# A new order for a chain of four layers: the first stage's steps, the pooling passes, and the end of the last batch

## The chip, the cores and the metric

The kernel runs on one core of one Trainium2 chip. The metric is the time of one execution on the device in microseconds (us); lower is better. TensorE is called PE here, VectorE DVE, ScalarE ACT, GpSimd POOL, and SyncE, whose queue issues the transfers, SP, as in the profile.

## The reference, cut to what matters

The input x has 4 batches of 512 channels by 64 x 64 pixels, all in fp32. Four layers follow one another:

```python
# layer 0: attention over 4096 pixels with 64 channels
t = einsum('oc,bchw->bohw', w_qkv, x)             # 3*64 x 512: key, query, value
attn = softmax(einsum('bdk,bdq->bkq', key, query), axis=1)
x = scale * einsum('oc,bchw->bohw', w_out, einsum('bdk,bkq->bdq', value, attn)) + x
# layer 1: experts mixed by a router of the pooled x, then 1x1, 3x3 and 1x1 convolutions
rw = sigmoid(x.mean(axis=(2, 3)) @ router_w.T + router_b)
x = relu(bn(conv(relu(bn(conv(relu(bn(conv(x, w1))), w2))), w3)) + x)
# layer 2: linear attention
Q, K, V = softplus(Wq x), softplus(Wk x), Wv x
x = x + gamma * (Q (K V)) / (Q sum(K))
# layer 3: gates and a scan
p = einsum('bchw,oc->bohw', x, w_proj) + b_proj   # 1024 x 512: gate and scan half
s = ds_cumsum(ds_cumsum(p_scan, discount, axis=2), discount, axis=3)
x = x + gamma * p_gate * sigmoid(s)
```

`ds_cumsum` is y_t = d * y_(t-1) + x_t along an axis.

## The kernel before, in words

A batch is 4096 pixels, cut into eight blocks of 512; two neighbouring blocks are a pair, so that there are four pairs of 1024 pixels. x lies in five places of 128 x 4 x 1024, one for each pair and a spare one that serves as scratch. `unshifted` does everything; a loop over the batches calls `layer0`, `layer1`, `layer2` and `layer3`. The instructions of PE are in the order in which the program writes them down, throughout. Those of DVE and ACT are so only inside a `with tc.manual_schedule(...)` block that names the engine; elsewhere a scheduler places them. SP's queue is worked off in order, and an instruction on it that waits holds up those behind it.

**Before the first batch.** SP loads the projection weights `wqkv_sb` (L99), the four pairs of x (L92, L94: the first two in four chunks each), then a table of small parameters `prm` (L105) and other weights. DVE adds two parts of `wqkv_sb` (L103) and works out the scale and shift of the batch norms from `prm` (L152 to L158), with a square root on ACT in between (L153). POOL makes the identity matrix and scales `wv_sb` and `bv_sb` by a factor from `prm` (L120, L121).

**The first stage of layer 0** (class `Projections`, L208 on) makes keys, queries and values. Keys and queries come from a scheme of seven products for two pairs at a time, which needs sums and differences of the input and of the weights in place of an eighth product. `steps` (L225) gives the order as a string, one word for a step; the first string is for pairs 0 and 1, the second for pairs 2 and 3:

- A digit is one of the seven products: four instructions on PE, which the profile counts as eight matmuls (L296). Products 1, 6, 7 and 4 collect in the bank `y` (in the profile kq); 5, 2 and 3 go to the two halves of `zy` (kqz).
- "seed" copies `y` to the first half of `zy` after product 1, "e2" and "e3" copy it out after products 6 and 7. They are ACT's (L301, L304), and the next product into `y` waits for them.
- "c11" copies finished keys out (ACT, four copies, L282), "c12" adds the keys of the second pair (DVE, L310) and then copies them to the other half of the partitions (ACT, two copies); "c21" and "c22" write queries (DVE, L313, L315).
- "t" and "n" with a digit are DVE's two sums for a product (L244, `ring` in the profile), for this pair of pairs and for the next one.
- "v" with a digit is the value projection of a pair (L252), with "a" or "b" a half of it; "cp" copies values out on ACT (L258), "tr" transposes them on PE (L265) and copies them on DVE (L269).
- "zero", in batch 0 alone, is a product of the identity with a stretch of `wqkv_sb` that clears a bank.

**The attention loop.** For each of four pairs of query blocks there are 32 key tiles. `scores` makes a 128 x 1024 tile on PE (L354) into one of three buffers, ACT takes the exponential into a ring of twelve (L357), DVE adds it to a running sum (L360, L362), and `values` multiplies it on PE (L369). The loop goes by groups of six tiles: first the six scores of a group, then the six values of the group before. In each of groups 2 to 9 stands one call of `pool`, a copy of x in place on ACT with a sum (L431): 8 passes a batch, for the pooled mean. They are free for the scheduler to place. After group 0 of batch 0, `router_of_values` transposes the output weights on PE, copies them on DVE (L173) and multiplies them by the router (L175).

**Layer 3** goes over eight tiles. A tile is a pair and two of four channel blocks, with seven products for the scan half (`Sums`) and seven for the gate half (`Gates`), all at L904. A turn of the loop at the end of `layer3` weaves three things: the products of the `Sums` of tile i (letter s), the products of the `Gates` of tile i-1 (letter g), and the scan of tile i-1 (letter l: "rows" on DVE, "turn" on ACT, "columns" on DVE, "sigmoid" on ACT, for each of two channel blocks). `steps`, `first_steps` and `last_steps` give the order: "s5" is product 5 of the sums, "s seed" the copy after product 1, "copy_out 2" and "copy_out 3" the copies after 6 and 7, as above. "y" and "a" are the last products and additions of layer 2, "q" takes the next of its remaining parts, whose last is `divide` (PE L760, DVE L763), "t" sums for the next tile or batch, "v" the value projection of pair 0 of the next batch, "x" the load of its pair 3, "d" the factors of the column scan. The last turn has no sums. `Gates.third` and `second` call `add_x` (L981), which multiplies a 128 x 1024 result by gamma, adds x on DVE (L983) and issues the store on SP (L984).

At the very end a check of the softmax sums (`cnt` on PE, `fits` on DVE) is loaded by every engine, SP among them, and decides whether a second kernel, `general`, has to run; it does not.

Of the kernel before, what the change touches and what calls it, by code (L numbers as in the profile page):

```python
# [10 lines left out]
ALU = mybir.AluOpType  # L11
# [4 lines left out]
P = 128  # L16
# [9 lines left out]
E = 8  # L26
# [19 lines left out]
def unshifted(ctx: ExitStack, tc: tile.TileContext, fits, x, wqkv_t, wout_t, router_t,  # L46
# [52 lines left out]
    nc.sync.dma_start(wqkv_sb, wqkv_t.rearrange("(kc p) o -> p kc o", p=P))  # L99
    xs = [load_pair(0, pr) for pr in range(NPAIR)]  # L100

    a11, a12, a21, a22 = (wqkv_sb[:, k:k + 2, w * D:(w + 1) * D] for w in range(2) for k in (0, 2))
    nc.vector.tensor_tensor(a21, a21, a22, ALU.add)  # L103
    prm_sb = const.tile([P, NPRM], F32, tag="prm", name="prm_sb")
    nc.sync.dma_start(prm_sb, prm)  # L105
    def col(i, n=1):
        return prm_sb[:, i:i + n]

    wout_sb = const.tile([P, C], F32, tag="wout", name="wout_sb")
    for h in range(2):  # L110
# [14 lines left out]
    ones = const.tile([P, P], F32, tag="ones", name="ones")  # L125
    nc.gpsimd.memset(ones, 1.0)


# [37 lines left out]
    def router_of_values():  # L166


        wo_t = pair_psum("wo_t")
        wot_sb = block("wot_sb")  # L170
        for kc in range(KC):
            nc.tensor.transpose(wo_t[:, 0, kc * P:(kc + 1) * P], wout_sb[:, kc * P:(kc + 1) * P], ident)
        nc.vector.tensor_copy(wot_sb, wo_t[:, 0, :])  # L173
        for kc in range(KC):
            nc.tensor.matmul(wo_t[:, 1, 0:E], wot_sb[:, kc * P:(kc + 1) * P], router_sb[:, kc, :],  # L175
                             start=kc == 0, stop=kc == KC - 1)
        nc.vector.tensor_scalar(wr_sb, wo_t[:, 1, 0:E], col(SCALE), 1.0 / HW, ALU.mult, ALU.mult)

# [29 lines left out]
    class Projections:  # L208
# [3 lines left out]
        def __init__(self, b):  # L212
            self.b = b
            self.sums = bigp.tile([P, 4, 2, NB], F32, tag="big", name=f"ring_{b}")
            self.fours, self.vv, self.vsb = [], {}, {}

# [8 lines left out]
        def steps(self, b):  # L225
            first = "v1 cp01 v2 5 1 seed t6 t4 n5 6 e2 2 c11 n6 tr01 7 e3 c22 v3a n7 4 c21 3 c12 n4"
            if b == 0:
                first = "zero v0 1 seed t5 v1 cp01 t6 5 2 c11 t7 t4 n5 6 e2 n6 tr01 v2 7 e3 c22 v3a n7 4 c21 3 c12 n4"
            return first.split(), "5 1 seed 6 e2 2 c11 v3b cp23 7 e3 c22 tr23 4 c21 3 c12".split()

# [42 lines left out]
        def products(self, xs, pair, steps, key, qry, vt):  # L273
# [10 lines left out]
            for step in steps:  # L284
                if y is None and (step.isdigit() or step == "zero"):
                    y, zy = bank(f"kq_{self.b}_{pair[0]}"), pair_psum(f"kqz_{self.b}_{pair[0]}")
                if step == "zero":

                    nc.tensor.matmul(zy[:, 0, :], ident, wqkv_sb.rearrange("p k o -> p (k o)")[:, 0:NB],
                                     start=True, stop=True)  # L290
                elif step.isdigit():
# [15 lines left out]
                elif step == "c12":  # L307
                    for h in range(2):
                        r, n0 = slice(h * D, (h + 1) * D), (2 * pair[1] + h) * NB
                        nc.vector.tensor_tensor(key[r, n0:n0 + NB], zy[r, 1, :], e["e2"][r, :], ALU.add)  # L310
                    to_key(lambda h, n0: key[h * D:(h + 1) * D, n0:n0 + NB], pair[1], own=False)
                elif step == "c21":
# [15 lines left out]
    def layer0(b, xs, pro):  # L328
# [93 lines left out]
        def out_step(pr, m):  # L422
            add_out(pr, m, out_product(pr, m))
# [10 lines left out]
        late = []  # L434
        for g, group in enumerate(groups):
            for i in group:
                scores(i)
            if 1 < g < 2 + 2 * KC:
                pool(NPAIR - 2 + (g - 2) // KC, (g - 2) % KC)
            if g == 0:  # L440
                if b == 0:
                    router_of_values()
                continue
            for _ in range(2):
                if late and late[0][0] < g:
                    late.pop(0)[1]()
            for n, i in enumerate(groups[g - 1]):
                if g == len(groups) - 1 and n == 4:
                    inverse_sums(NPAIR - 1)
                pr = values(i)  # L450
                if pr is not None:
                    late.append((g, lambda pr=pr: sums(pr)))
                    if pr < NPAIR - 2:
                        late += [(g + 1, lambda pr=pr, m=m: out_step(pr, m)) for m in range(KC)]
        assert not [t for t in late if t[0] < len(groups) - 1], late
# [396 lines left out]
    def layer3(b, xs, value_product, value_add, left, weights, wcq):  # L852
# [109 lines left out]
        class Gates(Block):  # L962
            def first(self):
                s = self.half(0, 0)
                nc.vector.scalar_tensor_tensor(s, self.zy[:, 0, :], self.bias[0], s, ALU.add, ALU.mult)

            def fourth(self):
                nc.vector.tensor_tensor(self.e[3], self.zy[:, 1, :], self.e[3], ALU.add)

            def third(self):  # L970
                s = self.half(1, 0)
                nc.vector.scalar_tensor_tensor(s, self.x, self.bias[1], s, ALU.add, ALU.mult)
                nc.vector.tensor_tensor(self.half(1, 1), self.half(1, 1), self.e[3], ALU.mult)
                self.add_x(1)

            def second(self):
                nc.vector.tensor_tensor(self.e[2], self.zy[:, 1, :], self.e[2], ALU.add)
                nc.vector.tensor_tensor(self.half(0, 1), self.half(0, 1), self.e[2], ALU.mult)
                self.add_x(0)

            def add_x(self, i):  # L981
                m, s = self.j + 2 * i, self.s[i]
                nc.vector.scalar_tensor_tensor(s, s, col(GAM3), xs[self.pr][:, m, :], ALU.mult, ALU.add)  # L983
                nc.sync.dma_start(out[b, m * P:(m + 1) * P, self.pr * 2 * NB:(self.pr + 1) * 2 * NB], s)  # L984

# [5 lines left out]
        steps = (("s1", "s seed", "l rows 1"), ("g1", "g seed", "y", "l rows 0", "l turn 1"),  # L991
                 ("s5", "l turn 0", "a", "q"), ("g5", "l columns 1"),
                 ("s6", "s copy_out 2", "l columns 0", "y"), ("g6", "g copy_out 2", "l sigmoid 1", "a"),
# [5 lines left out]
                       ("s3", "s second"))  # L999
        last_steps = (("g5", "l rows 1", "l rows 0"), ("g1", "g seed"), ("g6", "g copy_out 2", "l turn 1"), ("g2",),  # L1000
                      ("g7", "g copy_out 3", "l columns 1", "g fourth", "l turn 0", "l columns 0", "l sigmoid 1",
                       "l sigmoid 0", "v"), ("g4",), ("g3", "x", "g third", "g first", "g second"))
        pro = None
        ys = [(pr, m) for pr in range(1, NPAIR) for m in range(KC)]
        nxt = []
        with tc.manual_schedule(engines={mybir.EngineType.DVE, mybir.EngineType.Activation}):
# [9 lines left out]
            for i in range(len(tiles) + 1):  # L1016
                who = {"l": last, "s": Sums(1, i) if i < len(tiles) else None, "g": Gates(0, i - 1) if i else None}
                made = None
                for step in first_steps if i == 0 else steps if who["s"] else last_steps:
                    for what in step:  # L1020
                        name, *args = what.split()
                        if what[0] in "sg" and what[1:].isdigit():
                            if who[what[0]]:
# [23 lines left out]
                        elif name == "v" and pro:  # L1047
                            pro.value(nxt, 0)
                        elif name == "x" and pro:
# [469 lines left out]
```

## Time and profile before

| | us |
|---|---|
| time, median of 3 runs | 2700.67 (2700.61 to 2700.9) |
| the profiled execution: time / span | 2700.49 / 2698.4 |
| PE busy | 2650.6 |
| DVE busy | 2013.2 |
| ACT busy | 1318.2 |
| POOL busy | 11.8 |
| first product of PE starts | 4.38 |
| first scores of batch 0 start | 56.63 |
| first values of batch 0 start | 76.36 |
| first scores of batch 1 start | 730.50 |
| last product of PE starts | 2684.60 |
| last operation of DVE starts | 2691.93 |

The page gives each engine's busy time; the list of waits says which engine's instruction at which line waited for which, how long in total, how often and at most; the timeline gives the instructions in order with their start, their busy time and in brackets the idle time before them and what ended it. A busy PE can be a PE at half clock: the granted clock stands in its own row.

### The profile page before, as it was taken

Reading aid. Unit: us, or ns where it says so; the run is one execution under the profiler, and the core shown is the slowest. Engines: PE = TensorE matmul, PEld = TensorE weight load, DVE = VectorE, ACT = ScalarE, POOL = GpSimd, SP = SyncE. Lnnn points to the kernel's source line nnn. Section 1 sums busy time; section 2 is a strip of 40 time slices with the busy share of each in tenths; the row PEclk is TensorE's granted clock in tenths of the full one; section 3 lists DMA queues with packets and bytes.
Section 4 is the critical chain, followed back from the end, with each engine's and each line's share of the span. In section 5 each row is a group of like instructions: output and inputs, shape, how many; then the busy total and the mean of one; then the engine's idle time right before and its main releaser. Section 6 shows DMA issues by size and latency. Waiting matters only on the chain.

```text
span 2698.4 us, 25783 instructions
## 1 busy us (share of the span) xinstructions
PE 2650.6 (98%) x10048; PEld 1114.0 (41%) x10048; DVE 2013.2 (75%) x2270; ACT 1318.2 (49%) x1511; POOL 11.8 (0%) x26
## 2 busy tenths in 40 slices
PE   7999999999999999999999999999999999999998
PEld 2333365344333346434433334543443333554443
DVE  5678766788678876678877878668886777856787
ACT  4555353545655435345565453535556555353545
POOL 1000000000000000000000000000000000000000
PEclk9999999999999999999999999999999999999999
DMA  5000210022200021002220002001121000210011
GB/s 190 1 1 1 102 32 1 16 90 82 94 1 1 1 102 32 1 24 101 78 78 1 0 1 102 32 1 59 66 84 72 0 1 1 102 32 0 32 47 48
DMA packets 34595, 115.17 MB, mean 43 GB/s; under 512 B 2976, under 2 KB 12192, under 8 KB 32928
## 3 DMA queue, kind: packets, MB, share of 16 engines
q1 hardware_dynamic: 34464, 113.43, 11.2%
q8 instruction: 81, 1.33, 0.2%
q14 instruction: 50, 0.41, 0.0%
HBM read 79.86 MB, written 33.55 MB: 42 GB/s over the span
## 4 chain that ended last, share of the span: by engine, by line
PE 89%; DVE 5%; ACT 4%; DMA 1%; issue 1%; SPq 0%; DVEq 0%; ACTq 0%
PE av L369 17%; PE s L354 17%; PE sx L904 14%; PE zy L904 10%; PE z L648 4%; PE c L623 4%; PE c L551 4%; PE c L600 3%; PE wv L822 2%; PE y L413 2%; PE g L724 2%; PE xtr L709 2%; PE kq L296 2%; PE c2e L600 2%; PE vv L252 1%; DVE s L937 1%
## 5 line engine op out<-in xcount | busy, mean ns | idle before, releaser
L354 PE MATMUL s<-qv,key 64*128 64x512 f32 x2048 | 466.9, 602 | 3.4 <-ACT ring L357 3.4
L362 DVE TENSOR_TENSOR acc<-acc,ring 128x1024 f32<-128x1024 f32 x312 | 381.7, 1223 | 95.0 <-ACT ring L357 65.2
L357 ACT ACTIVATE ring<-s 128x1024 f32<-128x1024 f32 x336 | 317.1, 1039 | 210.6 <-PE s L354 210.6
L369 PE MATMUL av<-ring,qv 128*64 128x512 f32 x1344 | 304.5, 595 | 0.0
L354 PEld LDWEIGHTS s<-qv,key 64*128 64x128 f32 x2048 | 188.6, 187 | 279.5 <-issue 171.0
L362 DVE TENSOR_TENSOR acc<-acc,x 128x1024 f32<-128x1024 f32 x168 | 205.6, 1224 | 102.5 <-ACT x L357 89.5
L357 ACT ACTIVATE x<-s 128x1024 f32<-128x1024 f32 x176 | 171.7, 1040 | 203.2 <-PE s L354 203.2
L904 PE MATMUL sx<-t,x 128*128 128x512 f32 x512 | 237.7, 598 | 3.3 <-ACT zy L909 2.5
L369 PEld LDWEIGHTS av<-ring,qv 128*64 128x64 f32 x1344 | 93.3, 137 | 198.6 <-issue 198.6
L369 PE MATMUL av<-x,qv 128*64 128x512 f32 x704 | 167.2, 598 | 0.0
L909 ACT COPY zy<-sx 128x512 f32<-128x512 f32 x64 | 36.5, 570 | 265.8 <-PE sx L904 256.3
L904 PEld LDWEIGHTS sx<-t,x 128*128 128x128 f32 x512 | 95.1, 190 | 133.3 <-issue 117.4
L954 DVE TENSOR_TENSOR_SCAN t<-x,t 128x512 f32<-128x512 f32 x128 | 148.8, 1209 | 1.6
L943 ACT COPY t<-s 128x1024 f32<-128x1024 f32 x64 | 127.5, 1992 | 42.0 <-DVE s L937 41.4
L937 DVE TENSOR_TENSOR_SCAN s<-wc,s 128x512 f32<-128x512 f32 x128 | 146.0, 1202 | 0.0
L913 ACT ACTIVATE e<-sx,prm_sb 128x512 f32<-128x512 f32 x128 | 86.9, 685 | 108.6 <-PE sx L904 108.6
L960 ACT ACTIVATE s<-t 128x1024 f32<-128x1024 f32 x64 | 125.6, 1988 | 12.0 <-DVE t L954 12.0
L904 PE MATMUL zy<-t,wq 128*128 128x512 f32 x256 | 119.3, 604 | 0.0
L904 PE MATMUL sx<-t,wq 128*128 128x512 f32 x256 | 117.0, 597 | 2.1 <-ACT e L913 2.1
L904 PE MATMUL sx<-x,wq 128*128 128x512 f32 x256 | 117.1, 596 | 0.0
L904 PE MATMUL zy<-x,x 128*128 128x512 f32 x256 | 116.2, 594 | 0.0
L648 PE MATMUL z<-x,wqk_sb 128*64 128x512 f32 x512 | 115.9, 597 | 0.0
(229 smaller groups left out, 3443.6 us busy)
## 6 DMA issues: line engine op xcount, KB each, us to landing
out_dram<-s SPq DMA_DIRECT2D x64, 512.0 KB, 2.6
x<-in_x_dram SPq DMA_DIRECT2D x14, 2048.0 KB, 8.6
ex<-in_packed_dram SPq DMA_DIRECT2D x4, 2048.0 KB, 7.5
ex<-in_experts_dram SPq DMA_DIRECT2D x4, 2048.0 KB, 7.8
wq<-in_wproj_t_dram SPq DMA_DIRECT2D x32, 256.0 KB, 5.0
ex<-in_packed_dram SPq DMA_DIRECT2D x4, 1536.0 KB, 6.1
ex<-in_experts_dram SPq DMA_DIRECT2D x4, 1536.0 KB, 6.6
x<-in_packed_dram SPq DMA_DIRECT2D x4, 1536.0 KB, 8.3
```

The lines of the kernel that those rows point to most:

```text
L354: nc.tensor.matmul(s[:, h, :], key[r, kt * P:(kt + 1) * P], qry[r, pr * NB:(pr + 1) * NB], start=True, stop=True)
L357: nc.scalar.activation(p, s, AF.Exp)
L362: nc.vector.tensor_tensor(accs[pr], accs[pr], p, ALU.add)
L369: nc.tensor.matmul(avs[pr][h * D:(h + 1) * D, :], vt[:, kt, :], ring[i % RING][:, h, :], start=kt == 0, stop=kt == NT - 1)
L551: nc.tensor.matmul(y[:, h, :], wc[:, kc, :], xs[pr][:, kc, h * NB:(h + 1) * NB], start=kc == 0, stop=kc == KC - 1)
L600: nc.tensor.matmul(y[:, lo - a:hi - a], u, v[:, lo:hi], start=dy == 1, stop=dy == 2)
L648: nc.tensor.matmul(z[h * D:(h + 1) * D, i, :], wqk_sb[:, kc, w * D:(w + 1) * D], xs[pair[i]][:, kc, h * NB:(h + 1) * NB], start=kc == 0, s ...
L904: nc.tensor.matmul(y, w[:, c, self.kind, self.j * P:(self.j + 1) * P], v[:, c, :], start=c == 0 and k in (1, 5), stop=c == 1, skip_group_c ...
L937: nc.vector.tensor_tensor_scan(self.half(i, h), along[:, self.j + 2 * i, :], self.half(i, h), 0.0, ALU.mult, ALU.add)
L943: nc.scalar.copy(self.t[i].rearrange("p (w r) -> p w r", w=W), self.s[i].rearrange("p (r w) -> p w r", w=W))
L954: nc.vector.tensor_tensor_scan(th, down[:, i, :], th, 0.0, ALU.mult, ALU.add)
L960: nc.scalar.activation(self.s[i].rearrange("p (r w) -> p w r", w=W), tw, AF.Sigmoid)
```

## The change

It has these parts:

1. `prm` is loaded before x, and the sum of two parts of `wqkv_sb` is written down later. "zero" multiplies the identity by itself instead of a stretch of `wqkv_sb`.
2. The step strings of the first stage have a new order, for batch 0 and for the others. The copies behind "c12" are put off: those of the first two pairs to a new step "k", those of the last two to group 0 of the attention loop, after its six exponentials (`key_copies`).
3. The attention loop is put under `manual_schedule` for ACT, so that the pooling passes stay where they are written down. `router_of_values` leaves its products for the end of group 1.
4. In `steps` of layer 3 the "q" moves from s5 to behind g5. In `last_steps` the "v" is split: half of the value projection behind g1, half where it was.
5. For the last batch the last two turns become one, `end_steps`: the sums of the last tile (s), the gates of the last but one (g), and the gates of the last tile (h). The last tile's results are finished and stored in halves of 512 columns (`last`); those of g go through two POOL operations instead of one of DVE (`on_pool`).

The instruction lists show what goes with it: on PE, `cnt` stands behind the last product instead of between the last tile's products; on SP, four stores of 128 x 512 in place of two of 128 x 1024, and the stores of g stand between those of h. On SP the load of `fits` now has one store behind it; before, it had two.

```diff
@@ before the first batch
     nc.sync.dma_start(wqkv_sb, wqkv_t.rearrange("(kc p) o -> p kc o", p=P))
-    xs = [load_pair(0, pr) for pr in range(NPAIR)]
...
-    nc.vector.tensor_tensor(a21, a21, a22, ALU.add)
     prm_sb = const.tile([P, NPRM], F32, tag="prm", name="prm_sb")
     nc.sync.dma_start(prm_sb, prm)
...
+    xs = [load_pair(0, pr) for pr in range(NPAIR)]
...
     nc.gpsimd.memset(ones, 1.0)
+    nc.vector.tensor_tensor(a21, a21, a22, ALU.add)
@@ router_of_values
-        for kc in range(KC):
-            nc.tensor.matmul(wo_t[:, 1, 0:E], wot_sb[:, kc * P:(kc + 1) * P], router_sb[:, kc, :],
-                             start=kc == 0, stop=kc == KC - 1)
-        nc.vector.tensor_scalar(wr_sb, wo_t[:, 1, 0:E], col(SCALE), 1.0 / HW, ALU.mult, ALU.mult)
+
+        def products():
+            wr = pair_psum("wr_p")[:, 0, 0:E]
...
+        return products
@@ Projections.steps
-            first = "v1 cp01 v2 5 1 seed t6 t4 n5 6 e2 2 c11 n6 tr01 7 e3 c22 v3a n7 4 c21 3 c12 n4"
+            first = "v1 cp01 5 1 seed v2 t6 t4 n5 6 n6 e2 2 7 e3 c11 c22 tr01 n7 4 c21 3 c12 n4"
             if b == 0:
-                first = "zero v0 1 seed t5 v1 cp01 t6 5 2 c11 t7 t4 n5 6 e2 n6 tr01 v2 7 e3 c22 v3a n7 4 c21 3 c12 n4"
-            return first.split(), "5 1 seed 6 e2 2 c11 v3b cp23 7 e3 c22 tr23 4 c21 3 c12".split()
+                first = "zero v0 1 seed t5 v1 cp01 t6 5 2 t7 t4 6 e2 v2 7 e3 c11 c22 tr01 n5 n6 n7 4 c21 3 c12 n4"
+            return first.split(), "5 1 seed k v3a 6 e2 2 v3b cp23 7 e3 c11 c22 tr23 4 c21 3 c12".split()
+
+        def key_copies(self):
+            while self.left:
+                self.left.pop(0)()
@@ Projections.products
-                    nc.tensor.matmul(zy[:, 0, :], ident, wqkv_sb.rearrange("p k o -> p (k o)")[:, 0:NB],
-                                     start=True, stop=True)
+                    nc.tensor.matmul(zy[:, 0, :].rearrange("p (j c) -> p j c", c=P), ident,
+                                     ident[:, None, :].to_broadcast([P, TPB, P]), start=True, stop=True)
...
-                    to_key(lambda h, n0: key[h * D:(h + 1) * D, n0:n0 + NB], pair[1], own=False)
+                    self.left.append(lambda: to_key(lambda h, n0: key[h * D:(h + 1) * D, n0:n0 + NB], pair[1],
+                                                    own=False))
+                elif step == "k":
+                    self.key_copies()
@@ the attention loop
+        with tc.manual_schedule(engines={mybir.EngineType.Activation}):
+            for g, group in enumerate(groups):
...
+                if g == 0:
+                    pro.key_copies()
+                    if b == 0:
+                        router = router_of_values()
+                    continue
...
+                if b == 0 and g == 1:
+                    router()
@@ Gates (first, third and second now call add_x for each half)
+            last = on_pool = False
+
+            def add_x(self, i, h):
+                if h == 0 and not self.last:
+                    return
+                m = self.j + 2 * i
+                part = slice(h * NB if self.last else 0, (h + 1) * NB)
+                s = self.s[i][:, part]
+                if self.on_pool:
+                    nc.gpsimd.tensor_scalar(s, s, col(GAM3), None, ALU.mult)
+                    nc.gpsimd.tensor_tensor(s, s, xs[self.pr][:, m, part], ALU.add)
+                else:
+                    nc.vector.scalar_tensor_tensor(s, s, col(GAM3), xs[self.pr][:, m, part], ALU.mult, ALU.add)
...
@@ the orders of layer 3
-                 ("s5", "l turn 0", "a", "q"), ("g5", "l columns 1"),
+                 ("s5", "l turn 0", "a"), ("g5", "l columns 1", "q"),
...
-        last_steps = (("g5", "l rows 1", "l rows 0"), ("g1", "g seed"), ("g6", "g copy_out 2", "l turn 1"), ("g2",),
+        last_steps = (("g5", "l rows 1", "l rows 0"), ("g1", "g seed", "v 0"), ("g6", "g copy_out 2", "l turn 1"), ("g2",),
...
+        end_steps = (("s1", "s seed", "l rows 1"), ("g1", "g seed", "l rows 0", "l turn 1"), ("s5", "l turn 0"),
+                     ("s6", "s copy_out 2", "l columns 1"), ("g5", "l columns 0"),
+                     ("s2", "l sigmoid 1", "l sigmoid 0", "s first"), ("s7", "s copy_out 3", "s fourth"),
+                     ("g6", "g copy_out 2"), ("s4", "s third", "s rows 1", "d"),
+                     ("s3", "s second", "s turn 1", "s rows 0"), ("h1", "h seed", "s turn 0"), ("g2", "g first"),
+                     ("h5", "s columns 1"), ("g7", "g copy_out 3", "g fourth"),
+                     ("h6", "h copy_out 2", "s columns 0", "s sigmoid 1"), ("h2",), ("g4", "g third", "s sigmoid 0"),
+                     ("h7", "h copy_out 3", "h first", "h fourth"), ("g3", "g second"), ("h4", "h third"),
+                     ("h3", "h second"))
...
+                if b == B - 1 and i >= len(tiles) - 1:
+                    if i == len(tiles):
+                        break
+                    who["h"] = Gates(0, i)
+                    who["h"].last = who["g"].on_pool = True
```

## The prediction

> **What bounds the kernel now.** I read the page first: how busy each engine is.
>
> ```profile
> PE 2650.6 (98%) x10048; PEld 1114.0 (41%) x10048; DVE 2013.2 (75%) x2270; ACT 1318.2 (49%) x1511; POOL 11.8 (0%) x26
> ```
>
> TensorE (PE) is busy for all but 47.8 us of the 2698.4 us span. The change removes no product of weight, so it can only win gaps of PE, time in which PE runs at half clock, and the time after PE's last product. So the second view is the list of PE's waits over the whole run (us in total, times, longest).
>
> ```profile
> PE kq L296 <- ACT kqz L301: 7.5, 7, 2.8
> PE nrm L760 <- DVE x L827: 4.7, 4, 1.2
> ...
> PE kq L296 <- ACT e L304: 3.8, 5, 0.8
> PE s L354 <- ACT ring L357: 3.4, 4, 0.9
> PE wo_t L175 <- DVE wot_sb L173: 3.3, 1, 3.3
> ...
> PE sx L904 <- ACT zy L909: 2.5, 4, 0.7
> PE kqz L296 <- DVE qv L315: 1.8, 1, 1.8
> ```
>
> Seven, five and four times: the first stage of each of the four batches has the same small gaps, with larger ones in batch 0. The third view is the timeline of batch 0's start, PE, then ScalarE (ACT), then VectorE (DVE):
>
> ```profile
> 30.59 1.94 PE L296 MATMUL kq<-ring,wqkv_sb 128*64 128x512 f32 x8 [0.59 <-ACT e L304]
> 34.35 1.94 PE L296 MATMUL kqz<-x,kqw 128*64 128x512 f32 x8 [1.82 <-DVE qv L315]
> ...
> 42.57 3.51 PE L296 MATMUL kq<-ring,kqw 128*64 128x512 f32 x8 [2.85 <-ACT kqz L301]
> ```
> ```profile
> 28.43 0.21 ACT L153 ACTIVATE bn_s<-bn_v 128x6 f32<-128x6 f32 x1 [3.82 <-DVE bn_v L152]
> 28.66 1.28 ACT L331 ACT_TABLE_LOAD   x1
> 29.95 0.58 ACT L304 COPY e<-kq 128x512 f32<-128x512 f32 x1
> ```
> ```profile
> 26.97 1.23 DVE L244 TENSOR_TENSOR ring<-x,x 128x1024 f32<-128x1024 f32 x1 [5.45 <-DMA x<-in_x_dram]
> ...
> 34.21 4.08 DVE L244 TENSOR_TENSOR ring<-x 128x1024 f32<-128x1024 f32 x2
> ```
>
> See here: the copy e3 stands on ACT behind a square root, that behind bn_v on DVE, that behind the load of pair 3 (26.97). At 42.57 PE had waited 2.85 us and eight passes took 3.51 us, not 1.72. The last view is the end:
>
> ```profile
> 2684.60 1.92 PE L904 MATMUL zy<-x,x 128*128 128x512 f32 x4
> ```
> ```profile
> 2691.93 1.28 DVE L983 SCALAR_TENSOR_TENSOR s<-s,prm_sb,x 128x1024 f32<-128x1024 f32 x1
> ```
>
> PE ends at 2686.5, DVE at 2693.2; the last store is issued at 2693.3 and 5.1 us later the span ends.
>
> [...] The trace shows it after only 2.85 us: granted clock 0.50 from 43 to 45 us. [...] the first of the two sums at 34.21, beside POOL's 128x2048 scaling, took 2.94 us, the second 1.18. [...]
>
> **Batch 0's start, part by part.** Unit: a step of four instructions (eight passes) is 1.72 us, a value projection 3.43.
>
> - The clearing product "zero" needs only ident (POOL, done 1.4) instead of wqkv. No gain: PE then waits for the chunks of x, which came in at 8.01, 9.30, 10.58. A loss: PE is idle again until 6.3, so v0 starts at half clock. [...] I take 0.8.
> - prm moves ahead of x on SP's queue: everything behind it is one issue (0.5) and 25 KB later; I take 0.4 of delay (0.1 to 0.5).
> - The bn arithmetic and the square root go to the front of DVE and ACT. Cost nothing: DVE sits idle from 6.6 to 11.92 for x, ACT to 13.4. It takes 0.9 us and two table loads (2.6 us) off the stretch 23 to 32.
> - New step order, followed through: last chunk of pair 1 at 16.1, v1 to 17.0; 5, 2, 6 to 22.2; v2 to 25.6; 7 to 27.4; transposes to 28.3; 4, 3 to 31.7, no wait (copies e2, e3 of 0.58 now each have a product or the transposes beside them, and c22 comes at 28.0). Second pair: 5, 1, v3a to 36.9. Step 6 needs n6, and DVE does n5, n6, n7 only now: n5 to 32.2, then POOL's scaling (31.61 in the trace)[...], n6 to 38.4, so 6 ends at 39.3; 2, v3b to 42.7. Step 7 needs e2, queued on ACT behind the key copies "k", which need c12, on DVE behind n7 (40.7) and c21: 42.6, copies 43.25, e2 43.8. So 7 to 45.6, transposes, 4, 3 to 50.0. Scores start there, against 56.63.
> - Group 0: before, twelve scores and the router took 56.63 to 76.36 = 19.7 us, with waits of 0.85 and 3.35 us. The router's products now come a group later (0.5 us there); the two key copies (1.2) after exponential 5 make ACT fall behind by about a product. 12 x 0.905 + 0.55 + 0.4 = 11.8: values at 61.8, not 76.4.
>
> 14.5 - 0.5 - 0.8 = 13.2 us (10 to 15).
>
> **The pooling passes** (8 a batch, 1.06 + 0.19 us each) leave the first stage and go one to a group of the attention loop. Cost nothing: a group of six key tiles takes PE (466.9 + 471.7)/512 x 6 = 11.0 us, ACT's six exponentials 488.8/512 x 6 = 5.7. The pass comes after them, and the next scores are 5.5 us off.
>
> **The change of batch, three times.** Before, gaps of 0.66 (g seed), 0.67, 0.87, 0.79 and 0.85 us, and some 0.2 at each restart. In the new order v0's first half stands behind g1, v2 between seed and 6, v3a behind the second seed, "2" or v3b behind each e2, and ACT has no pooling passes. Followed through from the end of the last gate: scores start 4.0 us earlier, exponential 0 waits for nothing (+0.85), and the key copies after exponential 5 cost 0.7. 4.1 each (3 to 5), 12.4 together. n5 still waits for pair 3 (702.5) but is needed only at 709.7.
>
> **divide moved behind g5**, four times: nrm waited 1.18 us for a buffer that DVE frees at 2495.97; behind g5's 1.72 it is free. The product wv after it then waits about 0.3 for nrm's own buffer. 3.9 us in all (3 to 4.7).
>
> **The end.** 21 products of 1.72 from 2648.3. Copy_out 3 of the sums stands on ACT behind l sigmoid 0 (62.98) and s first, so s4 waits 2 us; PE ends at 2686.6 as before. But the chain rows, turn, columns, sigmoid now runs under h's products: s sigmoid 0 is done at 2680.9, and after h3 DVE has 2 to 3 us left. Against that, g's two results (g third done 2681.2) get gamma and x on POOL: twice a scaling and an add of 1024. Scaling: 6.2 us for 2048 and 1.92 for 512 give 3.35 on a line; [...] I take 2.8. [...] SP's order puts h's stores and the load of fits behind g's second store: three issues of 0.35 and 0.9 for fits, so the last issue is at about 2695.0 against 2693.3. A loss of 2 us[...]. cnt now comes after h3 and fits on DVE before three of h's last four operations: inside that count.
>
> **Sum**, against this execution (2698.4 span; it ran 2700.49, the three others 2700.61 to 2700.9): 13.2 + 12.4 + 3.9 - 2 = 27.5. 2700.67 - 27.5 = 2673.2.
>
> **Rivals.**
> - Half the first stage's gain: whatever ends a gap is followed by the next (n6 under POOL's scaling, "k" ahead of e2 on ACT, pair 3's load). For it: DVE's and ACT's queues are fixed, and my margins there are under 1 us. Against: most of the gaps before stand behind ACT work that leaves the stage. 13 us less: 2686.
> - POOL sets the end more dearly: adds and scalings of 3.35 us and more[...]. For it: the 2.94 us sum. End +8: 2679.
> - The end gains[...], and every gap closes: 2664.
> - Slower: the pooling passes hold up the exponentials, hence PE. 32 passes x 1.25 = 40 us against the 29.5 gained elsewhere than at the end: 2713. It decides from the point where ACT has under 1.25 us to spare in a group of six. Against: 5.3 us to spare.
> - The change does nothing: the gaps lie with loads. Only batch 0's first 17 us do; then about 2699.
>
> **How the numbers follow.** Forecast 0.55 (own range 2668 to 2679), half the gain 0.18, POOL's end 0.14, all gaps closed 0.08, slower 0.03, nothing 0.02. The range 2664 to 2684 leaves out the last two and a part of the half case. Faster by over 0.2% (5.4 us, about what a measurement of this kernel can tell from no change) has 0.95, within 0.02, slower 0.03.
>
> **What would show it.** Right: scores of batch 0 starting near 50 and their values near 62; no wait of kq for e or kqz of a microsecond; nrm without its 1.2; ACT's pooling passes between exponentials with no PE wait; four POOL instructions at the end, the last store behind them. Wrong: a clock of 0.5 in the first stage, waits of s for ring in the groups that pool, POOL instructions over 4 us, or kq waiting for ring sums between 32 and 45.

## The result, and the profile after

The changed kernel takes 2687.86 us (median of six, 2686.23 to 2688.84) against 2700.35 for the kernel before: a ratio of 0.9953, interval 0.9940 to 0.9966. It is 12.5 us faster, where 27.5 were forecast and the range ended at 2684. The profiled execution is the fastest of the six, 2686.23 with a span of 2684.4, so the two traces differ by 14.0 us.

The page's line of busy times for the changed kernel:

```profile
PE 2646.9 (99%) x10048; PEld 1113.4 (41%) x10048; DVE 2013.0 (75%) x2270; ACT 1314.6 (49%) x1510; POOL 23.9 (1%) x30
```

Its list of PE's waits (us in total, times, longest):

```profile
PE kqz L304 <- DVE qv L326: 6.2, 8, 0.8
PE sx L919 <- ACT e L928: 4.0, 9, 1.9
PE vv L260 <- DMA x<-in_x_dram: 3.9, 1, 3.9
PE s L365 <- ACT x L368: 3.1, 3, 1.0
...
PE kqz L304 <- DVE ring L252: 1.3, 1, 1.3
PE s L365 <- DVE wot_sb L173: 1.2, 1, 1.2
```

What the change aimed at is gone: kq waiting for kqz (7.5), for e (3.8), nrm (4.7) and wo_t (3.3; the scores now wait 1.2 us for the same copy `wot_sb`). But three other rows are new or grown. Kqz for qv was 1.8 us and is 6.2, eight times: it is product 3 of both halves of all four batches, waiting for c22. The scores wait for x, three times, at the key copies. Sx for e has one wait of 1.9, in the new end.

The timeline of batch 0's start, PE:

```profile
7.39 6.62 PE L260 MATMUL vv<-x,wqkv_sb 128*64 128x512 f32 x16 [3.87 <-DMA x<-in_x_dram]
...
33.12 1.94 PE L304 MATMUL kqz<-x,kqw 128*64 128x512 f32 x8 [0.76 <-DVE qv L326]
36.36 2.12 PE L304 MATMUL kqz<-ring,wqkv_sb 128*64 128x512 f32 x8 [1.30 <-DVE ring L252]
...
67.08 3.65 PE L380 MATMUL av<-ring,qv 128*64 128x512 f32 x16
```

and beside it ACT's four key copies c11, DVE's c22 and n5, and POOL's scaling:

```profile
29.99 2.35 ACT L290 COPY key<-kqz 64x512 f32<-64x512 f32 x4
```
```profile
32.38 0.69 DVE L326 TENSOR_TENSOR qv<-kqz,e 128x512 f32<-128x512 f32 x1 [10.30 <-PE kq L304]
...
34.18 3.17 DVE L252 TENSOR_TENSOR ring<-x,x 128x1024 f32<-128x1024 f32 x2
```
```profile
31.42 5.44 POOL L119 TENSOR_SCALAR wv_sb<-wv_sb,prm_sb 128x2048 f32<-128x2048 f32 x1 [29.95 <-DMA bv_sb<-in_bv_dram]
```

See three losses in a row: v0 takes 6.62 us, where the next two value projections take 3.62 (its passes take 1.06 us in the median instead of 0.59; that this is half clock was the author's reading, for the row of the granted clock reads 1.00 here); c22 starts only when c11 has ended (29.99 + 2.35); and n5, behind it, stands beside POOL. The first values start at 67.08, 9.3 us earlier than before, not 14.5.

The end, POOL, then the last of DVE, then the last of PE:

```profile
2664.99 2.85 POOL L1008 TENSOR_SCALAR s<-s,prm_sb 128x1024 f32<-128x1024 f32 x1 [265.31 <-DVE s L990]
2667.92 2.85 POOL L1009 TENSOR_TENSOR s<-s,x 128x1024 f32<-128x1024 f32 x1
2670.75 3.80 POOL L1008 TENSOR_SCALAR s<-s,prm_sb 128x1024 f32<-128x1024 f32 x1
2674.64 2.34 POOL L1009 TENSOR_TENSOR s<-s,x 128x1024 f32<-128x1024 f32 x1
```
```profile
2674.73 2.80 DVE L1011 SCALAR_TENSOR_TENSOR s<-s,prm_sb,x 128x512 f32<-128x512 f32 x1
```
```profile
2668.34 1.88 PE L919 MATMUL zy<-x,x 128*128 128x512 f32 x4
```

Two numbers split the 14.0 us of the traces. When product 1 of the last turn starts, the changed kernel is 17.2 ahead (2631.05 against 2648.29); from there to the end of the span it takes 53.35 instead of 50.1. So the last turn gives back 3.2.

### The profile page after: what moved, and what is told of

It reads as the page before. It is cut to its first block, busy times and chain, and to the rows that moved or that the text cites. A ratio compares the mean times of both kernels' runs of the same rounds, so it can differ in the third digit from the quotient of the medians.

```text
span 2684.4 us, 25795 instructions
## 1 busy us (share of the span) xinstructions
PE 2646.9 (99%) x10048; PEld 1113.4 (41%) x10048; DVE 2013.0 (75%) x2270; ACT 1314.6 (49%) x1510; POOL 23.9 (1%) x30
## 4 chain that ended last, share of the span: by engine, by line
PE 89%; DVE 5%; ACT 4%; issue 1%; DMA 0%; SPq 0%; ACTq 0%; DVEq 0%
PE av L380 17%; PE s L365 16%; PE sx L919 14%; PE zy L919 10%; PE z L663 4%; PE c L638 4%; PE c L566 4%; PE c L615 3%; PE wv L837 2%; PE y L424 2%; PE g L739 2%; PE xtr L724 2%; PE vv L260 2%; PE c2e L615 2%; PE kq L304 1%; PE kqz L304 1%
## 5 line engine op out<-in xcount | busy, mean ns | idle before, releaser
L975 ACT ACTIVATE s<-t 128x1024 f32<-128x1024 f32 x64 | 125.6, 1987 | 11.8 <-DVE t L969 11.7
L919 PE MATMUL zy<-x,wq 128*128 128x512 f32 x256 | 115.9, 592 | 0.0
```

The costliest lines, as they stand in the source:

```text
L919: nc.tensor.matmul(y, w[:, c, self.kind, self.j * P:(self.j + 1) * P], v[:, c, :], start=c == 0 and k in (1, 5), stop=c == 1, skip_group_c ...
L975: nc.scalar.activation(self.s[i].rearrange("p (r w) -> p w r", w=W), tw, AF.Sigmoid)
```

## The experiments

The experiments ran on three chips, each beside the kernel before: it took 2700.51 there for E1 to E4, 2699.90 for E5 and E7 to E9, and 2699.65 for E6 and E10 to E12. The changed kernel has one set of six times, beside 2700.35. The differences named below are differences of the times as they stand, and between chips up to 0.9 us of them can be the chip's. An interval of a ratio is about 3.5 us to either side; still, no run of E4 to E12 was as slow as the fastest of the changed kernel. The traces are compared by two numbers: where batch 0's first values start, and how long it is from there to the end of the span. The second leaves batch 0's start out.

| kernel | time, us | ratio to before, interval | first values | from there to the end |
|---|---|---|---|---|
| before | 2700.35 | | 76.36 | 2622.0 |
| changed | 2687.86 | 0.9953 (0.9940 to 0.9966) | 67.08 | 2617.3 |
| E1 c22 first | 2690.85 | 0.9968 (0.9956 to 0.9981) | 65.13 | 2620.0 |
| E2 clearing product four times | 2687.74 | 0.9953 (0.9939 to 0.9966) | 68.53 | 2617.8 |
| E3 prm later | 2686.96 | 0.9951 (0.9937 to 0.9964) | 68.49 | 2617.6 |
| E4 end on VectorE | 2685.01 | 0.9945 (0.9932 to 0.9959) | 69.23 | 2613.5 |
| E5 old end | 2683.88 | 0.9941 (0.9928 to 0.9955) | 69.68 | 2614.1 |
| E6 key copies later | 2682.30 | 0.9938 (0.9924 to 0.9951) | 69.06 | 2613.2 |
| E7 c11 early | 2683.06 | 0.9937 (0.9923 to 0.9950) | 68.51 | 2612.7 |
| E8 scaling on ScalarE | 2683.91 | 0.9942 (0.9929 to 0.9956) | 64.60 | 2617.5 |
| E9 = E7 + E8 | 2675.81 | 0.9915 (0.9902 to 0.9929) | 62.80 | 2611.1 |
| E10 = E9 + E4 + E6 | 2670.15 | 0.9892 (0.9877 to 0.9907) | 62.10 | 2605.4 |
| E11 = E10 + E3 + E12's order | 2666.38 | 0.9878 (0.9863 to 0.9893) | 61.60 | 2602.3 |
| E12 = E4 + copy ahead of sigmoid | 2682.90 | 0.9936 (0.9923 to 0.9950) | 69.24 | 2612.1 |

### E1, c22 ahead of c11

```diff
-  ... 7 e3 c11 c22 tr01 ...
+  ... 7 e3 c22 c11 tr01 ...        (all three strings)
```

> The changed kernel with one edit: in the three step strings c22 stands before c11. In the profile of the changed kernel c22 (DVE) starts each time when ACT's four key copies c11 end, and product 3 waits 0.77 us for c22, eight times. Theory A, c11 ahead of c22 is the cause: the eight waits (6.2 us, and some 0.2 at each restart) go, and in batch 0 the sums n5 to n7, which stand behind c22 on DVE, come 2.3 us earlier, so that product 5's wait of 1.3 us goes too: 7 to 10 us less than the changed kernel, that is 2678 to 2681. Rival, something else holds c22 or the next wait takes its place (key copies after exponential 5, n6 under POOL's scaling): 2 us less or nothing.

The median is 3 us slower than the changed kernel, and its six runs lie widely (2686.89 to 2695.92), for which the one trace, of the fastest run, gives no cause; that stays open. In batch 0 the half of theory A that concerns n5 came true: n5 starts at 30.91, takes 2.35 us, product 5 starts at 34.00 without a wait, and the values come 2 us earlier than in the changed kernel. From there on the trace is 2.7 us slower. PE's waits show what happened to product 3:

```profile
PE kqz L304 <- ACT key L290: 8.8, 8, 1.6
```

The eight waits are still there, and longer by 2.6 us in all; only the releaser has changed, from c22 to c11. Both copies read the tile zy, one its first half and one its second. Written in the order c11, c22, the second waits for the first (in the changed kernel's batch 0 c11 ends at 32.34 and c22 starts at 32.38); in the order c22, c11, product 3, which writes into zy, waits for c11 (0.91 us in batch 0). Product 3 waits for the last reader of the tile, whichever it is, and the four key copies (2.35 us) behind e3 make it late. That it is the shared tile which ties the two copies together is read from who releases whom in both orders; two separate tiles were not tried.

### E2, the clearing product issued four times

```diff
+  for _ in range(4):
       nc.tensor.matmul(zy[:, 0, :]..., ident, ident..., start=True, stop=True)
```

> The changed kernel with one edit: the clearing product zero is issued four times, so that PE is busy from 1.45 us until x arrives. Theory B, the first value projection lost its time to PE's halved clock after 3.9 us of idleness: its 16 passes end near 12.3 instead of 13.84 and all that follows comes 1 to 2 us earlier: 2686 to 2687. Rival, the chunks of x pace it: v0 ends where it did, and the time stays within 0.3 us.

PE is now busy from 1.45 to 7.83, and v0 takes 3.97 us instead of 6.62. Product 1 starts at 11.56, 2.3 us earlier than in the changed kernel's trace, whose v0 was a slow one: against the mean of ten traces with the same first instructions (12.76) it is 1.2, so about that is what the idle PE ahead of v0 costs. The time is unchanged, 2687.74, and the first values come at 68.53, later than in the changed kernel: product 5 of the second pair waits 3.13 us for n5 and starts at 36.10, as late as in the changed kernel (36.36).

### E3, prm behind the first two blocks of x

```diff
-  nc.sync.dma_start(prm_sb, prm)
-  xs = [load_pair(0, pr) for pr in range(NPAIR)]
+  xs = [load_pair(0, pr) for pr in range(2)]
+  nc.sync.dma_start(prm_sb, prm)
...
+  xs += [load_pair(0, pr) for pr in range(2, NPAIR)]
```

> The changed kernel with one edit: prm is loaded behind the chunks of pairs 0 and 1 instead of ahead of them. Theory C, the 25 KB in 128 short pieces cost the first chunk of x a microsecond (7.39 against at most 6.35 before): PE starts v0 1 us earlier, and the time falls by 0.5 to 1.2 us. Rival, the chunk was late for another reason, or the batch norm arithmetic, now behind t6 on DVE, holds up what follows: 0, or up to 1 us more.

V0 starts at 5.98 instead of 7.39, and product 1 at 11.27 instead of 13.84. The median is 0.9 lower, as theory C would have it, but the runs overlap (2685.78 to 2687.88 here), and in the trace nothing comes of the gain: product 5 waits 3.74 us for n5 and starts at 36.23, and the values come at 68.49. E2 and E3 together say that something pins that product at about 36 us, whatever PE wins ahead of it.

### E4, the closing additions on VectorE

```diff
-  who["h"].last = who["g"].on_pool = True
+  who["h"].last = True
```

> The changed kernel with one edit: on_pool stays False, so that g's two results of the last turn are finished by DVE in one operation each. Theory D, POOL's four operations (11.8 us one after the other) and the DVE operations that they block (four of 512 columns took 1.21, 1.99, 1.41 and 2.80 us instead of 0.67) set the end: DVE's last operation takes 0.7 us and the last store is issued 3 to 5 us earlier, so 3 to 5 us less: 2683 to 2685. Rival, the end is set by the chain of the last tile on DVE anyway, and two more operations of 1.28 us there cost as much as POOL did: within 1 us.

It is 2.9 us faster than the changed kernel, and the last turn takes 49.4 us instead of 53.35. Without POOL beside them DVE's four closing halves take 0.75 us each:

```profile
2677.23 0.75 DVE L1011 SCALAR_TENSOR_TENSOR s<-s,prm_sb,x 128x512 f32<-128x512 f32 x1
```

With POOL they took 1.21, 1.99, 1.41 and 2.80. After PE's last product DVE ends 5.5 us later instead of 7.3; and the last store is issued in the same moment (2678.0) instead of 1.9 us after DVE's end, where SP had still to send g's second store and to load fits (1.08 us). That makes 3.7 of the 4.0.

Its first stage is that of the changed kernel, and yet its values come 2.2 us later. PE is 1.75 us earlier at product 1 (12.09 against 13.84) and then waits longer:

```profile
37.01 3.31 PE L304 MATMUL kqz<-ring,wqkv_sb 128*64 128x512 f32 x8 [3.69 <-DVE ring L252]
```

The stretches of 2 us there (first the stretch and its length, then busy us and instructions of PE, weight loads, DVE, ACT and POOL, then the granted clock, the share of the DMA engines and GB/s):

```profile
36.00:38.00 2.00, 0.99 (x4) 0.23 (x4) 2.00 (x3) 0.00 (x0) 2.00 (x2) 0.86 0.02 8
38.00:40.00 2.00, 2.00 (x6) 0.79 (x6) 2.00 (x2) 0.00 (x0) 2.00 (x1) 0.50 0.00 0
```

The longer wait is followed by a granted clock of 0.50, and that costs another 1.7 us (products 5 and 1 take 3.03 and 2.12 us from start to start instead of 1.72). E4, E5, E6 and E12 have the same instructions up to the attention as the changed kernel, and in all four PE waits 2.0 to 3.9 us here, takes 5.1 to 5.4 us for products 5 and 1 together (in E6 too, whose clock was read, it was 0.50 from 38 to 40 us), and reaches the values at 69.1 to 69.7; E2 and E3, with waits of 3.1 and 3.7, do so at 68.5. The changed kernel's own trace has a wait of 1.30 and 67.08, which goes with its being the fastest of six executions.

### E5, the old end

```diff
-  if b == B - 1 and i >= len(tiles) - 1:
+  if False:
```

> The changed kernel with the old end: the last batch's last three blocks in the old order, whole outputs, the closing additions on VectorE. Theory E (the new end costs time: in the profile the changed kernel is 17.2 us ahead when the last turn begins and only 14.0 us ahead at the end of the span): 3.2 us faster than the changed kernel, about 2684.6, with PE ending about 12 us before the span does. Rival F (the end is as good as before, and the 3.2 us are a difference between the profiled execution and the others): within 1 us of 2687.9. The prediction's own term, a loss of 2, would give 2685.9.

2683.88, 4.0 below the changed kernel. The last turn takes 50.1, as it did before the change (2683.8 - 2633.71). So the new end as it stands loses 3 to 4 us, while the new order with DVE finishing (E4, 49.4) is 0.7 better than the old one by the traces; their times do not tell E4 from E5.

### E7, the key copies early

```diff
-  first:  ... 1 seed v2 t6 t4 n5 6 n6 e2 2 7 e3 c11 c22 tr01 ...
+  first:  ... 1 seed v2a t6 t4 n5 2 c11 6 n6 e2 v2b 7 e3 c22 tr01 ...
-  batch 0: ... 5 2 t7 t4 6 e2 v2 7 e3 c11 c22 tr01 ...
+  batch 0: ... 5 2 c11 t7 t4 6 e2 v2 7 e3 c22 tr01 ...
-  second: 5 1 seed k v3a 6 e2 2 v3b cp23 7 e3 c11 c22 tr23 ...
+  second: 5 1 seed k v3a 2 c11 6 e2 v3b cp23 7 e3 c22 tr23 ...
```

> In all three orders the four key copies (c11) stand right behind product 2 again, ahead of product 6's copy e2, and no longer between e3 and c22; nothing else moves but half of a value product (v2 split as v2a, v2b), put in front of product 2 in batches 1 to 3 to cover the seed. Theory B (product 3 waits for whichever of c11 and c22 reads the tile zy last, and the four copies are the late one): the eight waits of product 3, 6.2 us in the changed kernel, go to under 1 us in all, and the time falls by 5 to 6 us, to about 2682. Theory B with the pin (in batch 0 the first of these gains is eaten at product 5 of the second pair, which waits for the sums n5): 4.5 to 5.5 us, 2682.9. Rival C (c11 ahead of e2 delays e2, so that product 7 waits for it as in the kernel before, where kq<-kqz and kq<-e came to 11.3 us): a new wait of 0.5 to 1 us at each product 7 and about 2687 or slower.

2683.06, 4.8 faster. Of the eight waits of product 3 one of 1.0 us is left, in batch 2, where c22 stands on DVE behind n5 and n6, and n5 waits for the load of pair 3. From batch 0's values on it wins 4.6 us against the changed kernel. In batch 0 itself nothing is won, because the pin has moved:

```profile
46.63 3.68 PE L304 MATMUL kq<-ring,kqw 128*64 128x512 f32 x8 [3.37 <-ACT e L312]
```
```profile
42.37 1.34 ACT L290 COPY key<-key 64x512 f32<-64x512 f32 x2 [5.32 <-DVE key L318]
```

C22 is early now, so n5 runs before POOL starts (from 30.81, 2.35 us for its two sums), and it is n6 that stands beside POOL (5.79 us for its two). Behind n6 and n7 on DVE is c12, for c12 wait the key copies "k" on ACT, and behind "k" stand c11 and e2, for which product 7 waits 3.4 us; then it takes 3.61 us from start to start (46.63 to 50.24), where the same product took 1.82 in the changed kernel (46.89 to 48.71).

### E8, the scaling off POOL

```diff
-  nc.gpsimd.tensor_scalar(wv_sb, wv_sb, col(GAM2), None, ALU.mult)
-  nc.gpsimd.tensor_scalar(bv_sb, bv_sb, col(GAM2), None, ALU.mult)
...
+  if b == 0 and g in (12, 14):                      # in the attention loop
+      w = wv_sb[:, g - 12:g - 10, :].rearrange("p k c -> p (k c)")
+      nc.scalar.activation(w, w, AF.Copy, scale=col(GAM2))
+  if b == 0 and g == 13:
+      nc.scalar.activation(bv_sb, bv_sb, AF.Copy, scale=col(GAM2))
```

> POOL's two scalings of wv_sb and bv_sb (5.4 and 3.0 us from 31.4 us on) are removed and done on ScalarE in three passes of about 1 us, in groups 12 to 14 of batch 0's attention. Theory P (these scalings hold up VectorE's sums n5 and n6, and with them product 5 of batch 0's second pair, which then also runs at a lower clock): n5 takes about 2.4 us for its two, product 5 of the second pair starts without a wait for ring, batch 0's first values come 2 to 4 us earlier than the changed kernel's 67.1, and the time is 2684 to 2686. Rival Q (VectorE isn't held by POOL; n5 and product 5 are late for what stands before them): no change in the start, 2687.9; if the three passes hold up the exponentials, up to 3 us slower, with waits of s for x or ring in those groups.

2683.91, 4.0 faster. Product 5 of the second pair, and n5 and n6 on DVE:

```profile
33.88 2.12 PE L302 MATMUL kqz<-ring,wqkv_sb 128*64 128x512 f32 x8 [0.48 <-DVE ring L250]
```
```profile
32.52 2.35 DVE L250 TENSOR_TENSOR ring<-x,x 128x1024 f32<-128x1024 f32 x2
34.79 2.35 DVE L250 TENSOR_TENSOR ring<-x,ring 128x1024 f32<-128x1024 f32 x2
```

Both pairs of sums take 2.35 us, product 5 has 0.48 us of its wait left and starts 3 us earlier than in E4, the granted clock is 1.00 from 30 to 40 us, and the values start at 64.60, against 67.08 in the changed kernel's own trace and 69.1 to 69.7 in the four others. From there on nothing has changed (2617.5 against 2617.3): ACT's three passes, 1.19 us each for the two of 128 x 1024, hold up nobody. POOL's scaling was the pin.

### E9, both

> The two edits of the last two runs together: c11 right behind product 2, and the scalings on ScalarE. If theories B and P both hold and the pin is what hides part of the first in batch 0, the gains add up or a little more: 6 us for the waits of product 3 and 2 to 4 us for the pin, 2678 to 2680, and batch 0's first values at about 62 to 64 us. If C or Q holds for one of them, the time is that of the other alone.

2675.81, 12.1 faster than the changed kernel, more than 4.8 and 4.0 together and over 2 us more than was expected: each edit alone left batch 0's start to the other's cause. Kqz for qv and for ring are both gone from the list of waits.

### E6, the key copies in the second group

```diff
-  if g == 0:
-      pro.key_copies()
+  if g == 1:
+      pro.key_copies()
```

> The last two key copies of the second pair stand behind the exponentials of the attention's second group instead of its first; nothing else moves. Theory K (the two copies, 1.26 us together on ScalarE, stand between the sixth and seventh exponential and make the scores wait 1.04 us in each of batches 1 to 3; that is why the change of batch gains less than the prediction's 4.1 us each): the three waits of s for x, 3.1 us together, go, and the time falls by 3 us, to about 2685. Rival L (ScalarE makes the copies up only by delaying the next group: the wait moves and the time stays): 2687.9.

2682.30, 5.6 faster by the medians, 4.1 by the stretch after the values; 3 was expected. The trace explains most of its 4.1: in batch 1 the first values come 10.64 us after the first scores instead of 11.90, so a wait of 1.04 had cost 1.26 with its restart, and three of them 3.8. The rest of the 5.6 stays open. Batch 1's first twelve score tiles are now one run; in the changed kernel they were 36 and 12 matmuls with 1.04 us between them:

```profile
721.78 10.71 PE L365 MATMUL s<-qv,key 64*128 64x512 f32 x48
```

### E12, a copy ahead of a sigmoid in the end

```diff
-  ("s2", "l sigmoid 1", "l sigmoid 0", "s first"), ("s7", "s copy_out 3", "s fourth"),
+  ("s2", "l sigmoid 1", "s first"), ("s7", "s copy_out 3", "s fourth", "l sigmoid 0"),
```

> The changed kernel with the closing additions on VectorE (as in the fourth run) and, in the order of the end, the sums' copy s copy_out 3 ahead of the sigmoid l sigmoid 0 on ScalarE. Theory M (in the end's order product 4 of the last sums waits 1.85 us for that copy, which stands behind two sigmoids of 2.0 us and the copy s first): the wait goes, and the time is 1.5 to 1.9 us below the 2685.0 of the fourth run, about 2683.3; from the start of product 1 of the last turn to the end of the span 47.6 us instead of 49.4. Rival N (the copy isn't what bounds the end; the chain behind it, rows and sigmoids of the last sums on VectorE and ScalarE, is): PE waits later instead, 2685.0.

2.1 below E4, though on another chip: taken against the kernel before on its own chip, it is 1.25. Product 4 of the last sums, in the changed kernel and here:

```profile
2646.80 1.98 PE L919 MATMUL sx<-t,wq 128*128 128x512 f32 x4 [1.85 <-ACT e L928]
```
```profile
2647.02 1.88 PE L919 MATMUL sx<-t,wq 128*128 128x512 f32 x4
```

The wait is gone and doesn't come back later: the last turn takes 48.0 us, against 49.4 in E4 (47.6 was expected), and DVE's last addition ends 42.6 us after the turn's start instead of 44.7.

### E10 and E11, together

> The run with both edits of the first stage (c11 right behind product 2, the scalings on ScalarE; 2675.8), and with it the closing additions on VectorE and the key copies in the second group. If the four are independent: 2675.8 less 3 to 4 for the additions and less 3 for the copies, 2669 to 2670. If K is wrong, 2672 to 2673.

> The run before this one, and two more edits: the load of prm behind the first two blocks of x, and s copy_out 3 ahead of l sigmoid 0. With product 5 no longer held up by POOL, what the load of prm costs ahead of x should now show in the time: 1.0 to 1.4 us, as read from the third run's first 11 us; with M 1.5 to 1.9 us more: 2666 to 2667.5. If the load's cost is hidden still, 2667.5 to 2668; if M is wrong too, 2669.5.

2670.15 and 2666.38, as the sums of the single edits said. E11 is 33 us below the kernel before on its chip and 21 below the changed one. What each of its own two edits gave isn't told apart by the time; in the traces the scores start 0.9 us earlier than in E10 and the values 0.5, since the wait for wot_sb grows from 1.18 to 1.58. What its list of waits still has of single waits over a microsecond:

```profile
PE vv L259 <- DMA x<-in_x_dram: 2.3, 2, 2.1
...
PE s L364 <- DVE wot_sb L172: 1.6, 1, 1.6
PE kqz L296 <- POOL ident masks.py:199: 1.5, 1, 1.5
```

Its scores start at 48.42 and its values at 61.60; the forecast had 50.0 and 61.8.

## Why the prediction was wrong

The direction was right, and so was the list of gaps that would close. The size was not: the rival "half the first stage's gain", put at 0.18 and 2686, is what came, and by its own mechanism (what ends a gap is followed by the next). That it met the time so closely is partly luck: the followers that it named were n6, "k" and pair 3's load, and those that came in the changed kernel were c22 behind c11, and n5. Term by term, against the profiled execution:

| term | forecast | measured | |
|---|---|---|---|
| batch 0's start | 13.2 | 8.2 | 9.3 to the values, less 1.06 for wr_p behind them |
| change of batch | 12.4 | 3.9 | 1.3 each: batch 1's scores come 55.5 us after product 5 of the last gates, against 56.7, and the values 0.13 more |
| divide | 3.9 | 4.8 | four waits of nrm, some 1.2 each |
| the end | -2 | -3.2 | 53.35 against 50.1 |
| sum | 27.5 | 13.7 | 14.0 by the spans |

**"4, 3 to 31.7, no wait" and "c22 comes at 28.0".** This is the step that failed. It gave c22 only e3 to wait for. C22 stands behind c11 by a wait of the program, since both read zy, and so it came at 32.38: 2.35 us of that are c11's, the other 2.1 an e3 that was late already. In batch 0 that pushed n5 under POOL's scaling, and product 5, forecast at 31.7, started at 36.36. The same step was carried into every batch: two waits of 0.77 in each change of batch. Undoing it (E9 against the changed kernel, last gate's product 5 to batch 1's scores: 53.5 against 55.5 us) gives 2.0, so a wait of 0.77 costs 0.99 with its restart. Of the 4.0 forecast ahead of the scores 1.2 came, and 3.15 with it undone. Of the rest 0.22 is a wait for vsb that the new order brings; PE's change from one product shape to the value projection's and back, which the split of v makes once more, takes about 0.35 by the starts (665.98, 667.78, 669.65, 671.47); 0.3 stays open.

**Batch 0.** Product 1 starts at 13.84 in the changed kernel's trace, 2.35 later than before, where 1.2 were forecast for half clock and the load of prm. But v0 differs from one execution to the next, and this trace is the latest of ten with prm ahead of x and one clearing product; their mean is 12.76, 1.27 later than before, so the sum of the two terms was about right. The load alone was undersized: v0 starts at 7.0 in the mean of the ten, at 5.98 and 5.65 in the two traces with prm behind, so that it costs 1.2, outside the bounds of 0.1 to 0.5; only 0.6 of that shows, since before the change v0 started at 6.35, right behind the clearing product. E2 and E3 show that neither term is in the time, since n5 pinned product 5. Group 0 has a loss that the forecast didn't have: the scores wait 1.18 us for the copy of the transposed weights, so that 12.8 us pass from the first scores to the first values where 11.8 were forecast.

**"n5 to 32.2, then POOL's scaling".** That the scaling would hold up DVE's sums was foreseen, and the traces bear it out: the sum that meets POOL's scaling ends 0.65 us before the scaling does, whether it began at 31.61 (E3) or at 34.18 (the changed kernel), and two sums take up to 5.8 us against 2.35. What failed is the margin: n5 was to be done at 32.2, 0.6 us into the scaling, and with c22 4.4 us late it fell into the middle of it. The forecast hung on an order of events that would have held by less than a microsecond.

**Key copies after exponential 5.** 0.7 forecast, 1.04 measured as a wait and 1.26 with the restart (E6), three times. The mechanism was right, and E6 shows that one line would have avoided it.

**The end.** The chain was the forecast one, with a start 1.0 us late. Moved by the 17.2 us, POOL was to begin at 2664.0 and did so at 2665.0; its four operations took 12.0 to the end of the last addition, and from there to the last store 2.4 passed, so that this was issued at 2679.4, where 2677.8 was forecast (2695.0 less 17.2). How long POOL's additions would take was the author's estimate; the trace before has none. DVE's four halves, for which no delay was counted, took 4.4 us longer in all and ended 0.5 after POOL; the last store waited for SP in any case, whose queue kept its order: DVE's third half was done at 2673.4 and its store issued at 2677.4, behind g's second store, issued at 2677.0 when POOL was done. Product 4 of the sums waited 1.85 us where 2 was forecast, and E12 shows that wait to be avoidable.

**Right as forecast:** nrm, the pooling passes among the exponentials (no wait of s for ring in their groups), the first of POOL's scalings (2.85 against 2.8; the second took 3.80, more than the 3.35 on the line through the two scalings before), and SP's order with fits and the last store behind g's.

The range stopped short of that rival's time, 2686, which is the profiled execution's (2686.23). The median lies 1.6 above it; the four traces with the same instructions up to the attention, whose values come 2.0 to 2.6 us later, suggest why, though of the changed kernel itself only one execution was traced.

## What to carry to other kernels

- When a wait is taken away, work out what the waiting instruction's neighbours will wait for next, tile by tile: two readers of one tile in one order or the other, it is the last reader that the next writer waits for (product 3 for c22, 6.2 us in the changed kernel, and for c11, 8.8 in E1), and a change of their order is no cure (E1), while moving the long one ahead of the work that it would hold up is (E7).
- Work ahead of a pinned point is worth nothing until the pin is gone (E2, E3: 0 to 1 us; E7 and E8 alone 4.8 and 4.0, together 12.1). Look for the pin before the gaps in front of it.
- An idle engine isn't free when its work slows a busy one: beside POOL DVE's closing halves took 1.21 to 2.80 us, without it 0.75 (E4), and two sums beside the scaling up to 5.8 instead of 2.35. POOL took work off DVE at the end and cost 3 us by the times and 4.0 by the last turn (E4), and its 8.4 us at the start, for weights first used at 451 us (E8's trace), cost 4.0 (E8).

## What was not expected of the hardware

- Being early cost more than being late: E4, 1.75 us ahead of the changed kernel at product 1, was 2.15 behind it at the values. Behind a wait for n5 of 2.00 us (E6) and of 3.69 (E4) the granted clock of PE was 0.50 from 38 to 40 us, and products 5 and 1 took 1.7 us longer together than the 3.44 of E1. Behind 3.17 us (E5) and 3.90 (E12), where the clock wasn't read, they took 1.9 and 1.7 longer, and in E7, behind 3.37 us, product 7 and the transposes took 3.61 and 1.90 instead of 1.82 and 1.02. Behind the wait of 1.30 for n5 in the changed kernel the clock was 1.00 (36 to 40 us), and so it was behind the 1.85 in its end (2646 to 2650 us).
- The load of 25 KB ahead of x delayed the first product on x by about 1.2 us (7.0 in the mean of ten traces against 5.98 and 5.65).
- POOL's scaling of 128 x 1024 by a column of factors took 2.85 us and 3.80 in the same kernel; that of 128 x 2048 took 5.44 to 6.66, and the one after it, of 128 x 512, 2.98 (1.92 in the kernel before). The scaling took 6.63 and 6.66 us in E7 and E1, where DVE's sums were under way when it began, but 5.44 in the changed kernel, where DVE was idle then.
